# Attention and a selective scan on one core: GpSimd's products by pairs, the convolution spread over the step, the layer norm's scale and bias in the output projection, and two slots for its rstd

## The chip, the cores and the metric

The kernel runs on one core of a Trainium2 chip. Its time is the device time of one execution in microseconds; lower is better. The core has TensorE (PE, with its weight loads as PEld), VectorE (DVE), ScalarE (ACT), GpSimd (POOL), and SyncE (SP), which here issues all DMAs.

## What is computed

Two residual layers on an image batch `x` of 2 x 256 x 256 pixels with 128 channels, all in float32. Each begins with a group norm. The first is attention along the columns of the image. The second is a 3 x 3 convolution with a state space scan over all 65536 pixels of an image in row order; it takes most of the time and is what the change touches:

```python
def _L1_conv_ref(x, in_proj_w, conv_w, conv_b, x_proj_w, dt_w, dt_b, A_logs, Ds, ln_g, ln_b, out_proj_w):
    D_MODEL, D_INNER, D_STATE, DT_RANK = (128, 256, 16, 8)
    ...
    xz = x @ in_proj_w.T
    xi, z = jnp.split(xz, 2, axis=-1)
    xi = conv_3x3_depthwise(xi, conv_w) + conv_b
    xi = jax.nn.silu(xi)
    xs = xi.reshape(B, D_INNER, L)
    x_dbl = jnp.einsum('bdl,cd->bcl', xs, x_proj_w[0])
    dts, Bs, Cs = x_dbl[:, :8], x_dbl[:, 8:24], x_dbl[:, 24:]
    dts = jnp.einsum('brl,dr->bdl', dts, dt_w[0])
    delta = jax.nn.softplus(dts + dt_b[0][None, :, None])
    A = -jnp.exp(A_logs)
    y = selective_scan(xs, delta, A, Bs, Cs, Ds)
    # h = exp(delta * A) * h + (delta * xs) * B;  y = sum over 16 states of h * C, plus Ds * xs
    y = transpose_to_channels_last(y)
    mu, var = mean_and_variance(y)
    y = (y - mu) * jax.lax.rsqrt(var + 1e-05) * ln_g + ln_b
    y = y * jax.nn.silu(z)
    return y @ out_proj_w.T
```

(The convolution, the transposition and the moments are shown by names, and `x_dbl` is cut in one line.) Both layers add their result to their input.

## The kernel before

The attention stage runs first and leaves its result `x1` in HBM, one tensor for each image. The scan stage follows.

**Steps and units.** A *step* `k` is four image rows of one image, 1024 pixels (`R = 4`, `T = 1024`); there are 128, 64 for each image. In a step the scan has 256 channels x 16 states, that is 4096 recurrences, done 128 at a time: a *unit* has 32 channels (`q`, four of them in a half `h` of the channels) times 4 states (`m`, four groups), so a step has `NU = 32` units, and unit `t` is `(k, h, m, q)` with `q` running fastest. For each unit:

- `drive`: GpSimd multiplies `du` (delta times xs, spread to 128 partitions) by `bb` (the B rows, repeated) into `hb`;
- `decay`: ScalarE takes the exponential of `delta_r` times `a_neg` into `da`, in PSUM; two such tiles alternate, `da0` and `da1`;
- `scan`: VectorE runs the recurrence over 1024 pixels with `da` and `hb`, beginning from the last column that the step before left in `state`;
- `product`: the result times `cc` (the C rows), into `yc`. VectorE does it, but for the units of the tuple `POOLED`, where GpSimd does; there the scan writes into `hb` instead of `da`, since GpSimd reads no PSUM in this kernel;
- `remember`: ScalarE copies the last column to `state`;
- `add_up`, once for four units: TensorE sums the states of each channel with `sel`, into the PSUM tile `y`, where it has put `Ds * xs` at the beginning of a half; `y_out` copies `y` out at the end of a half.

**What feeds and follows it.** `project(k)` prepares step `k`: rows of `x1` are loaded (`raw`), transposed and normalised into `xn` (six rows, padded), convolved by nine accumulating matmuls for each of four blocks (`conv`, 512 pixels of one half of the channels each), gated (`gate`: z), and passed through silu, the x-projection (`states`), the dt-projection (`size`) and softplus; `times` multiplies delta by xs. `xs`, `delta`, `du`, `sz` and the B and C rows go to HBM and come back in the layouts of the units. `finish(k)` takes the step's four rows one by one: transposition and centring in one matmul (`turn`), sum of squares (`stats`), rstd on GpSimd (`scales`), `norm`, transposition back (`back`), the layer norm's scale and bias (`affine`), the product with silu(z) (`gated`, the one VectorE operation of a row), the output projection with the residual (`mix`) and the copy out (`leave`).

**Order.** The order on PE, ACT, DVE and POOL is written out by hand: a loop runs over slots `t`, one for each unit, and issues in each slot the pieces of the unit and then those pieces of `project` and `finish` that `at(t, piece)` has put there. In slot `t` these are `drive(t + 2)`, the GpSimd product of `t - 1` if it is pooled, `decay(t + 1)`, `scan(t)`, VectorE's product of `t`, `add_up(t - 5)` when its turn has come, the slot's pieces in the order in which they were put there, and `remember(t)`. SP is not in this order: the tile framework orders the DMAs that it issues. Every engine works its own queue strictly in order, so a piece that waits holds what stands behind it. In `project`, `base = k * NU - 2 * NU`: the convolution's 36 matmuls stand in slots 2 to 17 of a step, three to a slot, silu of xs in slot 21, the projections in slots 22 to 28, softplus in 29, silu of z in slot 1 of the next. The rows of `finish` begin at slots 3, 11, 19, 27 and put one piece in each slot.

**Buffers.** Tiles come from pools; a pool named `s3` has three buffers for each name. A tile whose buffers are all taken makes its writer wait for the last reader of the oldest. Here `bb` and `cc` have three, `xres` and `szr` two, `hb`, `delta_r` and `du_r` five, `yc` eight.

```python
    def pooled(t):
        return t % NU in POOLED
    ...
            if 0 <= t + 2 < end:
                drive(t + 2)
            if 0 <= t - 1 < end and pooled(t - 1):
                product(t - 1)
            if 0 <= t + 1 < end:
                decay(t + 1)
            if 0 <= t < end:
                scan(t)
                if not pooled(t):
                    product(t)
```

Of the kernel before, what the change touches and what calls it, by code (L numbers as in the profile page):

```python
# [15 lines left out]
P = 128  # L16
# [5 lines left out]
def attn_then_ssm_kernel(  # L22
# [92 lines left out]
    w_out = const.tile([P, NH, P], F32, name="w_out")  # L115
# [15 lines left out]
    with tc.tile_pool(name="prep", bufs=1) as prep, tc.tile_pool(  # L131
# [47 lines left out]
        for h in range(NH):  # L179
# [5 lines left out]
            transposed(w_out[:, h, :], outp[:, h * P : (h + 1) * P], P)  # L185
# [85 lines left out]
    with ExitStack() as actx:  # L271
# [207 lines left out]
        def gather(to, b, stats, layer):  # L479
            to[b] = group_stats(stats, ap, ps, f"{layer}_{b}", "t0")  # L480
# [102 lines left out]
    POOLED = (4, 7, 10, 13, 16, 19, 24, 26, 31)  # L583
    s1 = ctx.enter_context(tc.tile_pool(name="s1", bufs=1))
    s2 = ctx.enter_context(tc.tile_pool(name="s2", bufs=2))
    s3 = ctx.enter_context(tc.tile_pool(name="s3", bufs=3))
    s5 = ctx.enter_context(tc.tile_pool(name="s5", bufs=5))
    s8 = ctx.enter_context(tc.tile_pool(name="s8", bufs=8))
# [11 lines left out]
    def at(t, piece, *args):  # L600
        slots.setdefault(t, []).append((piece, args))

    halo = {}
    given = {}

    def project(k):
# [3 lines left out]
        base = k * NU - 2 * NU  # L610
# [4 lines left out]
        def load():  # L615

            o["raw"] = s1.tile([P, R, WT, C], F32, name="raw")
            nc.sync.dma_start(
                out=o["raw"][:, 0:n],
                in_=x1[b][R * s + 1 : R * s + 1 + n].rearrange("r (t p) c -> p r t c", p=P),  # L620
            )
            if s == 0:
                o["first"] = s1.tile([P, 1, WT, C], F32, name="first")
                nc.sync.dma_start(
                    out=o["first"], in_=x1[b][0:1].rearrange("r (t p) c -> p r t c", p=P)
                )

        def begin():


            xn = o["xn"] = s1.tile([P, R + 2, WP], F32, name="xn")
            nc.gpsimd.memset(xn[:, :, 0:1], 0.0)
            nc.gpsimd.memset(xn[:, :, WP - 1 : WP], 0.0)
            if s == 0:
                nc.gpsimd.memset(xn[:, 0, :], 0.0)
                turn("first", 0, 1)
                normalise(1, 1)
            else:
                nc.gpsimd.tensor_copy(xn[:, 0:2, 1 : W + 1], halo.pop(k - 1))
            if n < R:  # L640
                nc.gpsimd.memset(xn[:, 2 + n, :], 0.0)
# [9 lines left out]
        def normalise(to, m):  # L651
            nc.scalar.activation(
                o["xn"][:, to : to + m, 1 : W + 1],
# [6 lines left out]
        def keep():  # L660
            if s + 1 < NSTEP:
                halo[k] = s2.tile([P, 2, W], F32, name="keep")
                nc.gpsimd.tensor_copy(halo[k], o["xn"][:, R : R + 2, 1 : W + 1])

        def conv(h, i, dy):
            if dy == 0:
                o["u"] = ps_p.tile([P, RB, W], F32, name="u_ps", tag="p")
            for dx in range(3):
                nc.tensor.matmul(  # L669
                    o["u"],  # L670
                    w_tap[:, h, 3 * dy + dx, :],
                    o["xn"][:, i * RB + dy : i * RB + dy + RB, dx : dx + W],
                    start=(dy == 0 and dx == 0),
                    stop=(dy == 2 and dx == 2),
                )

        def conv_out(h, i):
            if (h, i) == (0, 0):
                o["xs"] = s1.tile([P, NH, T], F32, name="xs")
# [12 lines left out]
        def gate(h, i):  # L692
# [4 lines left out]
                o["xn"][:, 1 + i * RB : 1 + (i + 1) * RB, 1 : W + 1],  # L697
# [68 lines left out]
        at(base - 14, load)  # L766
        at(base - 4, begin)
        for r in range(0, n, RB):
            at(base - 3 + r, turn, "raw", r, min(RB, n - r))
            at(base - 2 + r, normalise, 2 + r, min(RB, n - r))  # L770
        at(base + 1, keep)
        t = base + 2
        for h in range(NH):
            for i in range(NB):
                for dy in range(3):
                    at(t + dy, conv, h, i, dy)
                at(t + 3, conv_out, h, i)
                at(t + 3, gate, h, i)
                at(t + 4, gate_out, h, i)
                t += 4  # L780
        t = base + 21
        at(t, silu_xs)
        at(t + 1, states, 0)
        at(t + 2, states_out, 0)
        at(t + 2, states, 1)
        at(t + 3, states_out, 1)
        t += 3
        for h in range(NH):
            for i in range(NB):
                at(t, size, h, i)  # L790
                at(t + 1, size_out, h, i)
                t += 1
        at(base + 29, softplus)
        at(base + 31, times, 0)
        at(base + NU, times, 1)
        at(base + NU + 1, silu_z)

    def finish(k):

        b, s = steps[k]  # L800
        for r in range(R):
            finish_row(k, b, R * s + r, r * W, (k + 1) * NU + 3 + r * (NU // R))

    def finish_row(k, b, row, t0, a):
        o = {}

        def fetch():
            o["xres"] = s2.tile([P, WT, C], F32, name="xres")
# [3 lines left out]
            o["szr"] = s2.tile([P, NH, W], F32, name="szr")  # L812
# [49 lines left out]
        def affine():  # L862
            for h in range(NH):
                nc.scalar.activation(  # L864
                    o["yd"][:, h, :],
                    o["yd"][:, h, :],
                    AF.Identity,
                    bias=lnb_c[:, h : h + 1],
                    scale=lng_c[:, h : h + 1],
                )  # L870

# [4 lines left out]
        def mix():  # L876
            o["o"] = ps_f.tile([P, WT, C], F32, name="o1_ps", tag="f")
            nc.tensor.matmul(o["o"], ident, o["xres"], start=True, stop=False)  # L878
            for j in range(WT):
                for h in range(NH):  # L880
                    nc.tensor.matmul(  # L881
                        o["o"][:, j, :],
                        o["yg"][:, h, j * P : (j + 1) * P],
                        w_out[:, h, :],
                        start=False,
# [194 lines left out]
```

## Time and profile before

| | |
|---|---|
| Time, median of 3 runs | 16465.56 us (16444.59 to 16481.3) |
| Profiled execution, its own time | 16465.48 us |
| Span of its instructions | 16463.4 us |
| First scan begins, last begins | 2690.5 us, 16402.8 us |
| Busy share of the span: DVE, POOL, PE, ACT | 90%, 83%, 83%, 67% |
| Busy from 2700 to 16400 us (13700 us): DVE, POOL, PE, ACT | 13193.7, 13336.8, 11200.3, 9583.1 us |
| Mean granted TensorE clock | 0.909; from 2700 to 16400 us 0.90 |
| DMA share of the 16 engines, 2700 to 16400 us | 0.67, 231 GB/s |

How to read it: busy rows by slice give tenths of 40 equal slices of the span (9 is 90% or more), `PEclk` the granted TensorE clock in tenths. A group line gives source line, engine, operation, what is written from what, shape and count, then the busy time in us, the mean of one in ns, and the idle time before it with what ended it. A line of the order of time gives start and duration in us, engine, source line, operation, tiles, count, and in brackets the idle time of the engine before it and its releaser. A line of waits gives who waited for whom, the us in total, how often, and the longest. A line of a stretch gives its bounds and length in us, and for PE, PEld, DVE, ACT and POOL the busy us and the number of instructions, then clock, DMA share and GB/s. Recorded durations of neighbours overlap by some hundredths of a microsecond, so distances between starts are the better measure of what one costs.

The time to landing of the loads that matter here, at the median: `bb` 4.2 us, `cc` 5.3, `delta_r` 5.6, `du_r` 4.1 (512 KB each), `xr` 7.2 (512 KB), `szr` 5.0 (256 KB), `xres` 3.7 (128 KB).

### The profile page before, as it was taken

The numbers are of one execution on the slowest core, as the hardware profiler recorded it, in microseconds if no ns is written. First come the engines' busy times: TensorE is split into PE (matmuls) and PEld (weight loads), VectorE is DVE, ScalarE is ACT, GpSimd is POOL, SyncE is SP. The second block draws the span as 40 slices with busy tenths as digits, with TensorE's granted clock in tenths as the row PEclk, the third lists the DMA queues.
The fourth block names the chain that finished last, engine by engine and source line by source line (L and its number), as shares of the span: only waits on it lengthen the run. The fifth ranks groups of instructions, "written<-read, shape, count | busy, mean of one in ns | idle before, by whom it ended". The sixth has DMA issues, their size and how long they took to land. (4 is left out here: it accounts for less than half of the span.)

```text
span 16463.4 us, 177150 instructions
## 1 busy us (share of the span) xinstructions
PE 13687.6 (83%) x55353; PEld 6810.9 (41%) x55353; DVE 14807.3 (90%) x12607; ACT 11039.0 (67%) x19870; POOL 13686.2 (83%) x7308
## 2 busy tenths in 40 slices
PE   6999997888888888888888888888888888888886
PEld 5777873333333333333333333333333333333333
DVE  7665555999999999999999999999999999999998
ACT  3555554677776677766777766777776767777665
POOL 0111114999999999999999999999999999999998
PEclk9999998888899888889998889999889998889997
DMA  4322224666666666666666666666666666666665
GB/s 186 131 86 88 82 83 146 232 234 230 232 234 230 233 232 232 233 229 232 233 233 231 233 228 232 232 235 231 230 229 230 234 234 231 233 230 234 230 231 171
DMA packets 1428932, 3452.05 MB, mean 210 GB/s; under 512 B 119784, under 2 KB 711184, under 8 KB 1407504
## 3 DMA queue, kind: packets, MB, share of 16 engines
q1 hardware_dynamic: 1427984, 3440.73, 60.6%
q8 instruction: 434, 7.11, 0.2%
q14 instruction: 514, 4.21, 0.1%
HBM read 2752.41 MB, written 687.88 MB: 209 GB/s over the span
## 5 line engine op out<-in xcount | busy, mean ns | idle before, releaser
L952 POOL TENSOR_TENSOR hb<-du_r,bb 128x1024 f32<-128x1024 f32 x4096 | 9575.1, 2363 | 0.0
L959 DVE TENSOR_TENSOR_SCAN da<-da,state,hb 128x1024 f32<-128x1024 f32 x2944 | 6903.2, 2345 | 327.8 <-ACT da L944 321.8
L944 ACT ACTIVATE da<-delta_r,a_neg 128x1024 f32<-128x1024 f32 x4096 | 4576.8, 1117 | 88.6 <-ACT state L964 0.8
L669 PE MATMUL u_ps<-xn,w_tap 128*128 128x512 f32 x9216 | 4230.3, 604 | 181.8 <-ACT state L964 168.2
L971 DVE TENSOR_TENSOR yc<-da,cc 128x1024 f32<-128x1024 f32 x2944 | 3604.7, 1224 | 254.9 <-DVE da L959 5.0
L971 POOL TENSOR_TENSOR yc<-hb,cc 128x1024 f32<-128x1024 f32 x1152 | 2719.6, 2361 | 203.0 <-issue 166.6
L959 DVE TENSOR_TENSOR_SCAN hb<-da,state,hb 128x1024 f32<-128x1024 f32 x1152 | 2697.3, 2341 | 72.6 <-ACT da L944 72.5
L991 PE MATMUL y<-yc,sel 128*32 128x512 f32 x16384 | 2527.4, 682 | 236.6 <-POOL yc L971 229.9
L669 PEld LDWEIGHTS u_ps<-xn,w_tap 128*128 128x128 f32 x9216 | 1718.3, 193 | 2190.5 <-issue 1781.4
L428 POOL TENSOR_TENSOR x1g<-xc,bo_all 128x512 f32<-128x512 f32 x256 | 315.9, 1273 | 1841.6 <-DVE stats L477 1839.7
L964 ACT COPY state<-da 128x1 f32<-128x1 f32 x2944 | 459.6, 156 | 1527.6 <-DVE yc L971 1525.8
L991 PEld LDWEIGHTS y<-yc,sel 128*32 128x32 f32 x16384 | 496.8, 116 | 1937.6 <-issue 1117.5
L821 PE MATMUL yt<-centre,ys 128*128 128x256 f32 x4096 | 1072.2, 407 | 218.4 <-ACT ob L891 217.4
L680 ACT ACTIVATE xs<-u_ps,cb_c 128x512 f32<-128x512 f32 x512 | 351.9, 687 | 1257.3 <-PE u_ps L669 977.9
L856 PE MATMUL yd<-ident,yn 128*128 128x128 f32 x2048 | 403.4, 331 | 906.5 <-ACT yn L845 877.5
L378 ACT ACTIVATE e<-s_ps,nmx 128x256 f32<-128x256 f32 x1024 | 477.6, 476 | 967.3 <-DVE nmx L369 955.1
L717 PE MATMUL xd_ps<-xs,w_xp 128*64 128x512 f32 x1024 | 683.5, 805 | 479.6 <-ACT state L964 374.8
L821 PEld LDWEIGHTS yt<-centre,ys 128*128 128x128 f32 x4096 | 794.2, 200 | 602.7 <-ACT ob L891 379.2
L735 PE MATMUL dt_ps<-xd,w_dt 8*128 8x512 f32 x1024 | 693.6, 761 | 270.7 <-ACT xd L730 263.9
L856 PEld LDWEIGHTS yd<-ident,yn 128*128 128x128 f32 x2048 | 291.2, 169 | 1263.8 <-ACT yn L845 916.2
L345 DVE TENSOR_TENSOR v<-v_ps,bv_all 128x512 f32<-128x512 f32 x256 | 177.0, 691 | 592.0 <-PE v_ps L338 592.0
L881 PEld LDWEIGHTS o_ps<-w_out,yg 128*128 128x128 f32 x4096 | 626.8, 219 | 41.4
(131 smaller groups left out, 17289.1 us busy)
## 6 DMA issues: line engine op xcount, KB each, us to landing
bb<-bc_d SPq DMA_DIRECT2D x1024, 512.0 KB, 4.2
cc<-bc_d SPq DMA_DIRECT2D x1024, 512.0 KB, 5.3
delta_r<-delta_d SPq DMA_DIRECT2D x1024, 512.0 KB, 5.6
du_r<-du_d SPq DMA_DIRECT2D x1024, 512.0 KB, 4.1
xs_d<-xs SPq DMA_DIRECT2D x128, 1024.0 KB, 6.9
xr<-xs_d SPq DMA_DIRECT2D x256, 512.0 KB, 7.2
delta_d<-delta SPq DMA_DIRECT2D x128, 1024.0 KB, 6.9
du_d<-xs SPq DMA_DIRECT2D x256, 512.0 KB, 3.2
```

Of the source, the lines that this page charges most:

```text
L378: nc.scalar.activation(e[:, i, :], o["s", r][:, i, :], AF.Exp, bias=o["nmx", r][:, i : i + 1], scale=SM, accum_out=o["den"][:, r, i : i + 1],)
L669: nc.tensor.matmul(o["u"], w_tap[:, h, 3 * dy + dx, :], o["xn"][:, i * RB + dy : i * RB + dy + RB, dx : dx + W], start=(dy == 0 and dx == ...
L717: nc.tensor.matmul(o["xd_ps"], w_xp[:, h, :], o["xs"][:, h, i * TB : (i + 1) * TB], start=(h == 0), stop=(h == NH - 1),)
L735: nc.tensor.matmul(o["dt"], w_dt[:, h, :], o["xd"][0:DR, i * TB : (i + 1) * TB], start=True, stop=True,)
L821: nc.tensor.matmul(o["yt"][:, j, :], ys[k, h][:, t0 + j * P : t0 + (j + 1) * P], centre[:, (1 - h) * P : (1 - h) * P + DI], start=(h == 0) ...
L856: nc.tensor.transpose(o["yd"][:, h, j * P : (j + 1) * P], o["yn"][:, j, h * P : (h + 1) * P], ident,)
L881: nc.tensor.matmul(o["o"][:, j, :], o["yg"][:, h, j * P : (j + 1) * P], w_out[:, h, :], start=False, stop=(j == WT - 1 and h == NH - 1),)
L944: nc.scalar.activation(da, spreads["delta", k, h, q], AF.Exp, scale=a_neg[:, g, m : m + 1])
L952: nc.gpsimd.tensor_tensor(hb, spreads["du", k, h, q], repeats["bb", k, h, m], ALU.mult)
L959: nc.vector.tensor_tensor_scan(u["h"], u["da"], u["hb"], st, ALU.mult, ALU.add)
L971: eng.tensor_tensor(u["yc"], u["h"], repeats["cc", k, h, m], ALU.mult)
L991: nc.tensor.matmul(y[q * CQ : (q + 1) * CQ, cols], sel, units[t + q]["yc"][:, cols], start=False, stop=(m == NSG - 1),)
```

## The change

**Pairs.** `POOLED` now names the first units of five pairs, so ten units of a step have their product on GpSimd instead of nine. GpSimd's drives are issued for two units at once (2048 elements a partition, `bb` and `cc` broadcast over the pair), in odd slots three units ahead, and its products for two units at once, two slots after the pair's first. `hb` and `du_r` become tiles of a pair with three buffers, `yc` of a pair with four; the buffers of `bb` and `cc` go from three to two.

**Timetable.** `base` is `k * NU - 72`. Each of the four convolution blocks gets eight slots: three, three, two and one of its nine matmuls in four successive slots, its copy out two slots later. Gates, projections and silus are put elsewhere: in slots of the step, silu of z in 21, silu of xs in 29, softplus in 13, `times` in 15 and 16. A slot's pieces are now kept in two lists, and those marked `pe=True` are issued after the others; `add_up` comes after both, a slot later than before, and `y_out` two slots later. `xn` is one tile for all steps; its two halo rows are copied by ScalarE within it, in place of two GpSimd copies by way of `keep`.

**Rows.** A row's slots begin at multiples of eight. `norm` comes two slots after `scales` instead of one. `affine` is gone: `w_out` holds the output weights twice, once times the layer norm's scale and once times its bias, and `mix` adds two matmuls for each block, `yg` with the first and silu(z) with the second. `xres` and `szr` have one buffer instead of two.

In the attention stage one call takes its small tiles from another pool.

```diff
-    w_out = const.tile([P, NH, P], F32, name="w_out")
+    w_out = const.tile([P, 2, NH, P], F32, name="w_out")
...
-            transposed(w_out[:, h, :], outp[:, h * P : (h + 1) * P], P)
+            for i, by in enumerate((lng_c, lnb_c)):
+                transposed(w_out[:, i, h, :], outp[:, h * P : (h + 1) * P], P)
+                nc.vector.tensor_scalar(
+                    w_out[:, i, h, :], w_out[:, i, h, :], by[:, h : h + 1], None, ALU.mult
+                )
...
-    POOLED = (4, 7, 10, 13, 16, 19, 24, 26, 31)
+    POOLED = (2, 6, 10, 18, 26)
...
-        base = k * NU - 2 * NU
+        base = k * NU - 72
...
-        def conv(h, i, dy):
-            if dy == 0:
+        def conv(h, i, taps):
+            if taps[0] == 0:
...
-        t = base + 2
-        for h in range(NH):
-            for i in range(NB):
-                for dy in range(3):
-                    at(t + dy, conv, h, i, dy)
-                at(t + 3, conv_out, h, i)
-                at(t + 3, gate, h, i)
-                at(t + 4, gate_out, h, i)
-                t += 4
-        t = base + 21
-        at(t, silu_xs)
...
-        at(base + 29, softplus)
-        at(base + 31, times, 0)
-        at(base + NU, times, 1)
-        at(base + NU + 1, silu_z)
+        CY = NU // 4
+        for c in range(4):
+            h, i = divmod(c, NB)
+            t = base + c * CY + 3
+            for dt, taps in ((0, (0, 1, 2)), (1, (3, 4, 5)), (2, (6, 7)), (3, (8,))):
+                at(t + dt, conv, h, i, taps, pe=True)
+            at(t + 5, conv_out, h, i)
+        for t, (h, i) in ((2, (0, 0)), (24, (0, 1)), (25, (1, 0)), (26, (1, 1))):
+            at(base + t, gate, h, i, pe=True)
+            at(base + t + 1, gate_out, h, i)
+        at(base + 29, silu_z)
+        at(base + 37, silu_xs)
+        for t, i in ((40, 0), (41, 1)):
+            at(base + t, states, i, pe=True)
+            at(base + t + 1, states_out, i)
+        for t, (h, i) in ((42, (0, 0)), (48, (1, 0)), (49, (0, 1)), (50, (1, 1))):
+            at(base + t, size, h, i, pe=True)
+            at(base + t + 1, size_out, h, i)
+        at(base + 53, softplus)
+        at(base + 55, times, 0)
+        at(base + 56, times, 1)
...
-            finish_row(k, b, R * s + r, r * W, (k + 1) * NU + 3 + r * (NU // R))
+            finish_row(k, b, R * s + r, r * W, (k + 1) * NU + (r + 1) * (NU // R))
...
-        def affine():
-            for h in range(NH):
-                nc.scalar.activation(
-                    o["yd"][:, h, :],
-                    o["yd"][:, h, :],
-                    AF.Identity,
-                    bias=lnb_c[:, h : h + 1],
-                    scale=lng_c[:, h : h + 1],
-                )
...
+                    for i, by in enumerate(("yg", "szr")):
+                        nc.tensor.matmul(
+                            o["o"][:, j, :],
+                            o[by][:, h, j * P : (j + 1) * P],
+                            w_out[:, i, h, :],
...
-        for i, piece in enumerate(
-            (turn, stats, scales, norm, back, affine, gated, mix, leave)
-        ):
-            at(a + i, piece)
+        for i, piece in (
+            (0, turn),
+            (1, stats),
+            (2, scales),
+            (4, norm),
+            (5, back),
+            (6, gated),
+            (7, mix),
+            (8, leave),
+        ):
+            at(a + i, piece, pe=piece in (turn, back, mix))
...
-                tl = repeats[name, k, h, m] = s3.tile([P, T], F32, name=name)
+                tl = repeats[name, k, h, m] = s2.tile([P, T], F32, name=name)
...
+        hb = s3.tile([P, 2, T], F32, name="hb")
+        units[t] = {"pair": hb, "hb": hb[:, 0, :]}
+        units[t + 1] = {"hb": hb[:, 1, :]}
+        nc.gpsimd.tensor_tensor(
+            hb,
+            spreads["pair", k, h, q],
+            repeats["bb", k, h, m].unsqueeze(1).to_broadcast([P, 2, T]),
+            ALU.mult,
+        )
...
+    def products(t):
+
+        k, h, m, q = unit(t)
+        hb = units[t]["pair"]
+        yc = s4.tile([P, 2, T], F32, name="yc")
+        for i in range(2):
+            units[t + i]["yc"] = yc[:, i, :]
+        nc.gpsimd.tensor_tensor(
+            yc, hb, repeats["cc", k, h, m].unsqueeze(1).to_broadcast([P, 2, T]), ALU.mult
+        )
...
-            if 0 <= t + 2 < end:
-                drive(t + 2)
-            if 0 <= t - 1 < end and pooled(t - 1):
-                product(t - 1)
+            if 0 <= t + 3 < end and t % 2:
+                drive(t + 3)
+            if 0 <= t - 2 < end and t % 2 == 0 and pooled(t - 2):
+                products(t - 2)
...
-            for piece, args in slots.pop(t, ()):
-                piece(*args)
+            for pieces in slots.pop(t, ()):
+                for piece, args in pieces:
+                    piece(*args)
+            if 0 <= t - 6 < end and (t - 6) % NQ == 0:
+                add_up(t - 6)
```

## The prediction

> **What bounds the kernel now.** I read the busy shares by slice first, then the costliest groups, then the order of time inside one step, and last who waits for whom.
>
> ```profile
> DVE  7665555999999999999999999999999999999998
> POOL 0111114999999999999999999999999999999998
> PEclk9999998888899888889998889999889998889997
> ...
> L952 POOL TENSOR_TENSOR hb<-du_r,bb 128x1024 f32<-128x1024 f32 x4096 | 9575.1, 2363 | 0.0
> ...
> L971 DVE TENSOR_TENSOR yc<-da,cc 128x1024 f32<-128x1024 f32 x2944 | 3604.7, 1224 | 254.9 <-DVE da L959 5.0
> L971 POOL TENSOR_TENSOR yc<-hb,cc 128x1024 f32<-128x1024 f32 x1152 | 2719.6, 2361 | 203.0 <-issue 166.6
> ...
> L428 POOL TENSOR_TENSOR x1g<-xc,bo_all 128x512 f32<-128x512 f32 x256 | 315.9, 1273 | 1841.6 <-DVE stats L477 1839.7
> ```
>
> From slice 7 on VectorE and GpSimd are both nine tenths busy. This is the scan stage: 128 steps of 32 units, from the first scan at 2690.5 us to the end of the last at 16405.1, 13714.6 us or 107.15 a step. GpSimd's drives (L952) never wait; its products (L971) do. To see which engine is late, I price a step from the distances between starts:
>
> ```profile
> 5009.58 2.36 DVE L959 TENSOR_TENSOR_SCAN da<-da,state,hb 128x1024 f32<-128x1024 f32 x1
> 5012.04 1.22 DVE L971 TENSOR_TENSOR yc<-da,cc 128x1024 f32<-128x1024 f32 x1
> 5013.18 2.34 DVE L959 TENSOR_TENSOR_SCAN hb<-da,state,hb 128x1024 f32<-128x1024 f32 x1
> 5015.44 2.33 DVE L959 TENSOR_TENSOR_SCAN da<-da,state,hb 128x1024 f32<-128x1024 f32 x1
> ...
> 5030.72 2.36 DVE L959 TENSOR_TENSOR_SCAN da<-da,state,hb 128x1024 f32<-128x1024 f32 x1 [1.29 <-ACT da L944]
> ...
> 5035.86 2.36 DVE L959 TENSOR_TENSOR_SCAN da<-da,state,hb 128x1024 f32<-128x1024 f32 x1 [1.45 <-ACT da L944]
> ```
>
> A unit with its product on VectorE takes 3.60 us here (3.57 averaged over a step's unpooled units), one with the product on GpSimd ("pooled") 2.26, a row's gating 0.60. VectorE: 23 x 3.57 + 9 x 2.26 + 4 x 0.60 = 104.8 us a step. GpSimd's 1024-wide products follow each other at 2.315 us; with 0.92 a row for the rstd pair, 0.57 for each halo copy and 0.1 of memsets: 43 x 2.315 + 3.7 + 1.2 = 104.5. The rest of the 107.15 is VectorE waiting for ScalarE's decay:
>
> ```profile
> DVE da L959 <- ACT da L944: 173.0, 316, 2.0
> DVE hb L959 <- ACT da L944: 72.5, 38, 2.4
> DVE yc L971 <- DVE da L959: 5.0, 11, 0.5
> ```
>
> That is 245 us, 1.9 a step; GpSimd costs VectorE 2 us in all. These stalls sit at units 29 to 31 (up to 2 us each, in 36 long steps of 108 to 112 us) and at unit 8 (0.6 us in many steps). Why is ScalarE late? In the long step above:
>
> ```profile
> 5007.05 1.93 PE L717 MATMUL xd_ps<-xs,w_xp 128*64 128x512 f32 x4 [3.07 <-ACT state L964]
> ...
> 5018.19 3.64 PE L991 MATMUL y<-yc,sel 128*32 128x512 f32 x16
> ...
> 5033.76 1.92 PE L991 MATMUL y<-yc,sel 128*32 128x512 f32 x16
> ```
> ```profile
> 5023.87 0.69 ACT L746 ACTIVATE delta<-dt_ps,dtb_c 128x512 f32<-128x512 f32 x1 [3.44 <-PE dt_ps L735]
> ```
> ```profile
> 5015.00:5030.00 15.00, 13.88 (x36) 5.72 (x36) 13.90 (x9) 7.57 (x15) 14.35 (x9) 0.50 0.63 202
> 5060.00:5105.00 45.00, 43.65 (x161) 18.63 (x163) 43.86 (x26) 26.18 (x53) 43.80 (x23) 1.00 0.67 232
> ```
>
> After the packed convolution TensorE idles (3.07 us here), its clock falls to 0.50, the same 16 matmuls take 3.64 us instead of 1.92, and ScalarE, which reads its queue in order, waits 3.44 us for a step size before it can issue the next decay. At unit 8 the opposite: TensorE has 43.65 of 45 us full of convolution, and the gate comes late. So VectorE bounds, GpSimd stands 0.3 us behind it, TensorE's timing makes the stalls.
>
> **The change, per step.** *Products.* 22 instead of 23 on VectorE: 22 x 3.57 + 10 x 2.26 + 2.4 = 103.5, 1.3 less. On GpSimd 32 drives and 10 products become 21 pairs of 2048. No such width is in the trace. From 512 to 1024 wide it goes from 1273 to 2361 ns, 2.125 ns an element, so 4.54 us; less the 0.045 by which neighbours overlap, 4.49 from start to start, against 4.63 for two singles. The ends are 4.63 (no saving) and 4.45: the Trainium skill, "GPSIMD Engine Reference", section 3.1, gives 4497 ns for a tensor_tensor of 2048 f32. I take 4.49. GpSimd: 21 x 4.49 + 2 x 2.315 + 3.7 = 102.6 (101.8 to 105.5), the halo having gone to ScalarE. Section 4.1 of that page speaks against the change: elementwise belongs on VectorE, GpSimd being about twice as slow. Its rows agree (2361 against 1224 ns) and by the rule alone a product moved loses 1.1 us; here it takes 1.3 off the later engine and the pairs pay for it.
>
> Do the pairs fit in time? Between scan 2 and scan 20 GpSimd must run 8 drives, 3 products, both `du` products and an rstd: 11 x 4.49 + 4.63 + 0.92 = 54.9; VectorE has 8 pooled and 10 plain units and 2 gatings, 55.0. It fits with nothing over; afterwards the lead grows again. An rstd or a half-speed TensorE that comes late there costs VectorE some tenths.
>
> *Convolution spread*, eight units for each of four blocks. TensorE's work at full clock is about 18.7 us in each 26 us (18 convolution passes at 0.44, `y` 1.9, `yt` 1.7, the mix now 2.3, the rest). Weighed against it: the skill's "TensorE: Matmul & The Clock Gate", section "HAM oscillation", wants the matmuls dense, since idle stretches beyond about 3.4 us drop the clock. The packed stretch at 1.00 agrees; spread too thin, all 81 us of a step at half clock would be over 160, TensorE would bind and the step with it. But its longest wait becomes some 2 us, and at 3.98 us busy of 5 the trace kept 1.00: I expect 0.97 or more, and both kinds of stall to go. I keep 0.7 us a step for what GpSimd's tight stretch and ScalarE leave: 104.2. If the cover fails, the 1.9 stay.
>
> *Scale and bias into the projection:* ScalarE loses 8 x 0.53 us a row group, 4.2 a step, and gains the 0.58 halo copy; neither is on the path, ScalarE being 70% busy. TensorE gains 16 small matmuls, 3.5 us, inside its slack. *Silus and softplus* move to units 13, 21, 29: table load, 1.91, table load, decay is 5.6 us against two plain units of 7.1 plus a gating: covered. *Rstd one unit more:* norm comes later, gating not until two units after it: nothing.
>
> *Fewer buffers.* `cc` (and `bb`) have two: SP's load of `cc` for the group after next waits for the last product before it, five times a step GpSimd's. Queued behind on SP: two or three `delta` loads, `xr`, `xres`, needed three units later. Between that product's end and VectorE's need lie one drive and one scan, 4.49 + 2.4 = 6.9 us; the load lands in 5.3 at the median: nothing. `xres`, `szr` with one buffer are fetched six units ahead, 5.0 to land: nothing.
>
> *Ends.* Before the first scan, step 1's states and sizes (2668 to 2687) move behind it: -19. In the four rows after the last scan (12.2 us each) -1.1 for the affine, +1.9 for the mix at half clock: +3. Preparing the second weight: +1.
>
> **Sum.** 128 x (104.2 - 107.15) = -378; -378 - 19 + 4 = -393. The span of 16463.4 becomes 16070; its own time is 2.1 us above it, so 16072. That execution (16465.5) stands at the median of the runs, nothing to correct.
>
> **Rivals.**
> - *GpSimd binds:* a pair costs two singles. 105.5 + 0.5: -147 - 15, 16303. For it: a broadcast operand at this width is not in the trace. Against: L428, broadcast too, shows the fixed part. 0.14.
> - *The stalls stay* (ScalarE late for another reason, or the clock stays low): 103.9 + 1.9 = 105.8, 16280. Against: every long stall has a late TensorE before it. 0.11.
> - *Slower:* `cc` lands late. Five sites a step lie 6.9 us after a GpSimd product; each microsecond beyond costs 5. From 7.5 us it eats the gain; at 8.0, 5.5 a step, 109.7 and 16775. For it: `xr`, of equal size, takes 7.2. Against: `cc` takes 5.3 with the same traffic, and a paced GpSimd gives more time than 6.9. 0.08.
> - *Hardly anything:* GpSimd's own waits (3 us a step now) come on top of 103. 0.03.
>
> My forecast has 0.64. Faster 0.88, within 0.2% (33 us, about what a measurement here tells apart) 0.03, slower 0.09. Range: low end with no stalls left (103.5) and the ends, 15980; high end takes in the first two rivals, 16310.
>
> **What would show it.** GpSimd pairs near 4.5 us; VectorE's waits for `da` under 80 us in all; granted clock at 0.97 or more; a step near 104; no `yc` on VectorE waiting for `cc`. Wrong, if drives run without a gap while scans wait for `hb` (first rival), if waits for `da` stay at 240, or if products wait for a DMA.

## The result, and the profile after

The changed kernel takes 16219.45 us (median of 4 runs, 16216.73 to 16221.97) against 16473.43 (16444.59 to 16482.11, 4 runs): ratio 0.9849, 95% interval 0.9832 to 0.9866. It is 254 us faster where 393 were forecast. The span of the profiled execution is 16220.2 us.

The page of the kernel after, busy tenths and the costliest groups:

```profile
DVE  7665555999999999999999999999999999999998
...
POOL 1111114999999999999999999999999999999998
PEclk8999998999999999999999889999999999999998
...
L957 POOL TENSOR_TENSOR hb<-du_r,bb 128x2048 f32<-128x2048 f32 x2048 | 9266.3, 4542 | 71.3 <-DMA du_r<-du_d 15.4
...
L983 DVE TENSOR_TENSOR yc<-da,cc 128x1024 f32<-128x1024 f32 x2816 | 3449.3, 1225 | 423.5 <-PE y L1014 257.4
...
L992 POOL TENSOR_TENSOR yc<-hb,cc 128x2048 f32<-128x2048 f32 x640 | 2906.7, 4542 | 62.3 <-ACT delta L747 46.8
```

The pairs last 4542 ns, drives and products alike, and GpSimd now idles 71.3 us before its drives, where it had 0.0. But the products on VectorE (L983) have 423.5 us of idle time before them where there were 254.9, most of it behind TensorE's `y`. The waits of VectorE from 2700 to 16100 us (who waited for whom, us in total, times, longest):

```profile
DVE yc L983 <- PE y L1014: 257.4, 297, 2.0
DVE da L969 <- POOL hb L957: 30.2, 98, 1.0
DVE hb L969 <- ACT da L947: 15.3, 2, 13.3
DVE yc L983 <- DMA cc<-bc_d: 11.3, 17, 1.7
```

Of the 245 us that VectorE waited for the decay, 15 are left, and 13.3 of these are one single wait, in the step that begins the second image. **In their place stands a wait that was not there: products wait for TensorE's sum.**

Between the first scan's start and the last one's end lie 13488.0 us, 105.38 a step (13714.6 and 107.15 before). I split this time into waits of VectorE (its gaps over 0.15 us, each counted whole) and the rest, its work:

| us | before | after | predicted difference | measured |
|---|---|---|---|---|
| VectorE's work in the scan stage | 13455.8 | 13168.6 | 128 x -1.3 = -166 | -287 |
| its waits there | 258.8 | 319.4 | 128 x (0.7 - 2.35) = -211 | +61 |
| up to the first scan, behind the last, preparation | 2690.5 + 58.2 | 2672.9 + 59.3 | -15 | -16.5 |
| span | 16463.4 | 16220.2 | -393 | -243 |

**Where the wait for the sum comes from.** `yc` has four pair buffers, so unit 12's product writes where units 4 and 5 wrote, and needs the sum over those to have been read: `add_up(4)`, which slot 10 issues. By the change it stands behind that slot's TensorE pieces. These end a chain of small matmuls, each of which waits until ScalarE has copied out the one before it. The order of time in a step of the kernel after (start, us, engine, line; in brackets the idle time and its releaser), TensorE first and then VectorE:

```profile
7952.98 1.92 PE L1014 MATMUL y<-yc,sel 128*32 128x512 f32 x16
...
7959.70 1.12 PE L736 MATMUL dt_ps<-xd,w_dt 8*128 8x512 f32 x2
7961.60 1.12 PE L736 MATMUL dt_ps<-xd,w_dt 8*128 8x512 f32 x2 [0.78 <-ACT delta L747]
7963.86 2.07 PE L736 MATMUL dt_ps<-xd,w_dt 8*128 8x512 f32 x2 [1.14 <-ACT delta L747]
7965.86 3.64 PE L1014 MATMUL y<-yc,sel 128*32 128x512 f32 x16
```
```profile
7961.78 4.58 DVE L969 TENSOR_TENSOR_SCAN hb<-da,state,hb 128x1024 f32<-128x1024 f32 x2
7966.28 2.33 DVE L969 TENSOR_TENSOR_SCAN da<-da,state,hb 128x1024 f32<-128x1024 f32 x1
7969.54 1.23 DVE L983 TENSOR_TENSOR yc<-da,cc 128x1024 f32<-128x1024 f32 x1 [0.93 <-PE y L1014]
```

and the same stretch by 2 us (bounds and length; busy us of PE, PEld, DVE, ACT, POOL; then the granted clock, DMA share, GB/s):

```profile
7960.00:7962.00 2.00, 1.22 (x3) 0.29 (x2) 1.97 (x3) 1.44 (x6) 1.92 (x2) 1.00 0.00 0
7962.00:7964.00 2.00, 0.86 (x3) 0.14 (x1) 2.00 (x1) 1.78 (x3) 2.00 (x1) 0.72 0.64 246
7964.00:7966.00 2.00, 2.00 (x6) 0.50 (x10) 2.00 (x2) 1.24 (x3) 1.83 (x3) 0.50 0.93 341
```

TensorE is busy for 1.22 and 0.86 of 2 us, its clock falls to 0.50, and the last pair of the chain takes 2.07 us instead of 1.12, the sum 3.64 instead of 1.92. At full clock, by my estimate, the sum would end 0.95 + 1.72 = 2.67 us earlier than 7969.50, and the product, due 2.38 us after its scan's start (7968.66), would not wait. Two scans without a product come before it (units 10 and 11 are pooled), which is why there is no slack here. The mean over the 112 steps between 3000 and 15000 us repeats this in three places: the clock is 0.53, 0.51 and 0.50 in units 11, 19 and 27, behind the step sizes, the gates, and the transpositions of new rows with a gate, and 0.96 or more in the twenty-three units outside 10 to 12, 18 to 20 and 26 to 28; units 12, 20 and 28 take 4.39, 3.89 and 4.34 us where others of their kind take 3.52 to 3.64.

### The profile page after: what moved, and what is told of

Its sections match the earlier page's. It is cut to its first block, busy times and chain, and to the rows that moved or that the text cites. A ratio compares the mean times of both kernels' runs of the same rounds, so it can differ in the third digit from the quotient of the medians.

```text
span 16220.2 us, 178642 instructions
## 1 busy us (share of the span) xinstructions
PE 14005.8 (86%) x59451; PEld 7034.3 (43%) x59451; DVE 14617.8 (90%) x12483; ACT 10627.5 (66%) x18973; POOL 13488.7 (83%) x4240
## 5 line engine op out<-in xcount | busy, mean ns | idle before, releaser
L957 POOL TENSOR_TENSOR hb<-du_r,bb 128x2048 f32<-128x2048 f32 x2048 | 9266.3, 4542 | 71.3 <-DMA du_r<-du_d 15.4
L969 DVE TENSOR_TENSOR_SCAN da<-da,state,hb 128x1024 f32<-128x1024 f32 x2816 | 6607.3, 2346 | 164.7 <-ACT da L947 131.5
L983 DVE TENSOR_TENSOR yc<-da,cc 128x1024 f32<-128x1024 f32 x2816 | 3449.3, 1225 | 423.5 <-PE y L1014 257.4
L969 DVE TENSOR_TENSOR_SCAN hb<-da,state,hb 128x1024 f32<-128x1024 f32 x1280 | 2946.7, 2335 | 15.9 <-ACT da L947 15.9
L992 POOL TENSOR_TENSOR yc<-hb,cc 128x2048 f32<-128x2048 f32 x640 | 2906.7, 4542 | 62.3 <-ACT delta L747 46.8
L695 PE MATMUL z_ps<-xn,w_z 128*128 128x512 f32 x1024 | 801.3, 875 | 696.1 <-ACT sz L706 424.0
L819 PEld LDWEIGHTS yt<-centre,ys 128*128 128x128 f32 x4096 | 744.6, 192 | 691.1 <-ACT ob L880 607.6
L870 PE MATMUL o_ps<-w_out,szr 128*128 128x128 f32 x4096 | 797.7, 277 | 0.0
L870 PE MATMUL o_ps<-w_out,yg 128*128 128x128 f32 x4096 | 796.6, 276 | 0.0
L764 POOL TENSOR_TENSOR xs<-delta,xs 128x1024 f32<-128x1024 f32 x256 | 598.7, 2364 | 98.3 <-ACT delta L755 98.3
```

Of the source, the lines that this page charges most:

```text
L695: nc.tensor.matmul(o["z"], w_z[:, h, :], xn[:, 1 + i * RB : 1 + (i + 1) * RB, 1 : W + 1], start=True, stop=True,)
L764: nc.gpsimd.tensor_tensor(du, o["delta"][:, h, :], du, ALU.mult)
L819: nc.tensor.matmul(o["yt"][:, j, :], ys[k, h][:, t0 + j * P : t0 + (j + 1) * P], centre[:, (1 - h) * P : (1 - h) * P + DI], start=(h == 0) ...
L870: nc.tensor.matmul(o["o"][:, j, :], o[by][:, h, j * P : (j + 1) * P], w_out[:, i, h, :], start=False, stop=(j == WT - 1 and h == NH - 1 an ...
L957: nc.gpsimd.tensor_tensor(hb, spreads["pair", k, h, q], repeats["bb", k, h, m].unsqueeze(1).to_broadcast([P, 2, T]), ALU.mult,)
L969: nc.vector.tensor_tensor_scan(u["h"], u["da"], u["hb"], st, ALU.mult, ALU.add)
```

## The experiments

Each is the kernel after with one edit, unless it says otherwise; ratios are to the kernel before. The kernel before itself stood between 16437 and 16482 us on the chips used, so differences of some 20 us are read from the waits, not from the ratio.

**1. The pairs taken apart:** each of GpSimd's instructions of two units becomes two of one unit, drives and products (shown) alike.

```diff
-        nc.gpsimd.tensor_tensor(
-            yc, hb, repeats["cc", k, h, m].unsqueeze(1).to_broadcast([P, 2, T]), ALU.mult
-        )
+        for i in range(2):
+            nc.gpsimd.tensor_tensor(
+                yc[:, i, :], hb[:, i, :], repeats["cc", k, h, m], ALU.mult
+            )
```

> GpSimd's pairs taken apart: drives and products as two 1024-wide instructions each, in the same slots and order. If the pair saves about 0.14 us and GpSimd stands close behind VectorE, GpSimd's step grows by 21 x 0.14 = 2.9 us to about 105.5 plus its own waits, VectorE waits for hb for over 100 us in all, and the time is 16330 to 16500. Rival: VectorE and TensorE's y alone set the step and GpSimd has 2.6 us to spare: within 30 us of 16219.

16422.47 us, 0.9981 (0.9973 to 0.9988): 203 us of the gain are the pairs. VectorE's work stays (13169.2 us); its waits in this run:

```profile
DVE yc L981 <- DMA cc<-bc_d: 283.3, 151, 4.1
DVE yc L981 <- PE y L1013: 195.0, 178, 2.2
...
DVE da L967 <- POOL hb L958: 9.1, 17, 1.0
```

GpSimd without pairs is late (106.6 us of work a step, from start to start), but this hardly shows as scans waiting for `hb`. It shows as products waiting for `cc`, most of them (239 us) in unit 28. One of these waits, SP first and then VectorE:

```profile
3919.05 0.60 SPq L933 DMA_DIRECT2D du_r<-du_d  x1
3927.90 0.51 SPq L919 DMA_DIRECT2D bb<-bc_d  x1
...
3929.65 1.53 SPq L919 DMA_DIRECT2D cc<-bc_d  x1
```
```profile
3938.95 1.23 DVE L981 TENSOR_TENSOR yc<-da,cc 128x1024 f32<-128x1024 f32 x1 [3.94 <-DMA cc<-bc_d]
```

The buffer of `cc` itself is free in good time: VectorE's product of unit 23, its last reader, starts at 3919.94. But SP stands from 3919.65 to 3927.90 at a load of `bb`, whose buffer a late drive of GpSimd still reads, and the load of `cc` is queued behind it. At the median of 100 steps it is issued 7.6 us after its own buffer came free (5.6 in the kernel after). So this is the prediction's first rival, come by the door of its third, though through `bb` and SP's queue and not, as the third had it, behind a product of GpSimd.

**2. Four pooled pairs** instead of five.

```diff
-    POOLED = (2, 6, 10, 18, 26)
+    POOLED = (2, 10, 18, 26)
```

> Four pairs instead of five (units 6 and 7 back on VectorE). If VectorE sets the step: two more products, 2 x 1.29 us a step, less the 0.24 us that it waits for hb now: some 300 us more, 16520. Rival, GpSimd sets the step: it loses 4.5 us of work a step, so faster, 16100 or less.

16503.45 us, 1.0031 (1.0019 to 1.0042). Two products more on VectorE make its work 13489.4 us, +321 or 2.51 a step (two times 1.28 is 2.56, the working being 3.53 - 2.25); waits for `hb` are gone and those for `y` stay at 261. VectorE sets the step: GpSimd has 4.7 us less to do in it, and the kernel is slower.

**3. The sum first:** `add_up` before the slot's TensorE pieces, behind the others.

```diff
-            for pieces in slots.pop(t, ()):
-                for piece, args in pieces:
-                    piece(*args)
+            acts, pes = slots.pop(t, ((), ()))
+            for piece, args in acts:
+                piece(*args)
             if 0 <= t - 6 < end and (t - 6) % NQ == 0:
                 add_up(t - 6)
+            for piece, args in pes:
+                piece(*args)
```

> add_up issued before the slot's TensorE pieces instead of behind them, same slot. If VectorE's 257 us of waiting for y come from the place behind them: these waits fall below 60 us, the time by 200 to 250 us, to about 15990. Rival: the pieces now stand behind the sum, ScalarE gets its step sizes and gates later and the waits for da return (over 100 us): within 60 us of 16219. Second rival, the sum is late because its own inputs are (GpSimd's products): waits for y unchanged.

16159.23 us (16152.93 to 16185.95), 0.9825 (0.981 to 0.9839). Its waits of VectorE:

```profile
DVE da L969 <- POOL hb L957: 71.8, 91, 1.1
DVE yc L983 <- DMA cc<-bc_d: 53.7, 84, 1.6
DVE da L969 <- ACT da L947: 47.0, 67, 1.8
DVE hb L969 <- ACT da L947: 25.0, 11, 13.9
```

No product waits for `y`: the order was the cause. (The clock rises too, to 0.944 in the scan stage and from 0.51 to 1.00 in unit 19, so this run alone does not tell the place of the sum from the clock behind which it stood; run 4 does so in part.) But of 257 us only some 60 are gained, where 200 to 250 were expected. Other waits grew by 151 (in the whole scan stage: GpSimd's drives and `cc` by 84, the decay by 57, a row's `yd` by 9), and VectorE's work by 43; units 12, 19 and 28 are still 0.4 to 0.7 us long. A faster VectorE runs into GpSimd. The prediction had given it 0.9 us a step less to do than VectorE; from start to start it has 103.6 us of work against VectorE's 102.9 in the kernel after, and it waits 87.6 us here for ScalarE's `yn` before its rstd.

**4. Fuller chains:** gates and step sizes are each issued twice, to keep TensorE busy (the second overwrites the first with the same value).

```diff
-            nc.tensor.matmul(o["dt"], w_dt[:, h, :], ..., start=True, stop=True)
+            for _ in range(2):
+                nc.tensor.matmul(o["dt"], w_dt[:, h, :], ..., start=True, stop=True)
```

> Each gate and each step-size matmul is issued twice into the same tile (the second overwrites the first with the same values), so that TensorE has more to do in the slots where its clock falls. If the half clock at units 10 to 12, 18 to 20 and 26 to 28 makes y late: clock at 0.96 or more, waits for y below 80 us, time about 16020. Rival, TensorE has simply too much before the sum: clock up or not, the waits for y grow by the added 1 us at these units, time 16300.

17007.8 us, 1.0333 (1.0318 to 1.0349): a miss in size and sign. At the gates the clock rose from 0.51 to 1.00 and unit 20 no longer waits (3.57 us). At the step sizes, matmuls of 8 rows of the array, it was 0.92, 0.51, 0.59 in units 10 to 12, no better than 0.80, 0.53, 0.61 after unit 10, and there the doubled work only lengthens the chain (unit 12: 7.24 us). In the whole scan stage the waits for `y` are 698 us and those for the decay 334. That the sum is not late at full clock is shown at one of three places, whose share of the 257 us was 45; filling with matmuls, as tried here, is no remedy.

**5. Nine taps in one slot** instead of 3, 3, 2 and 1 in four.

```diff
-            for dt, taps in ((0, (0, 1, 2)), (1, (3, 4, 5)), (2, (6, 7)), (3, (8,))):
+            for dt, taps in ((0, tuple(range(9))),):
```

> The nine matmuls of a convolution block all in the first of its four slots; everything else as in the changed kernel. If spreading them keeps TensorE fast and in time: 8 us of convolution in one slot, idle stretches after it, clock below 0.91, the waits of VectorE for y, yd or da grow from 315 us to 500 or more, time 16400 to 16700. Rival, with three quarters of its time in use TensorE absorbs it: within 60 us of 16219.

16287.44 us, 0.9899 (0.9882 to 0.9915): 68 us more, near the rival's bound. Waits for the decay stay at 15, those for `y` rise to 290 and for `cc` to 30; VectorE's work grows by 35. Spreading one block's taps over four slots is worth these 68 us, a quarter of the gain, and the stalls for the decay do not come back without it.

**6. Scale and bias back on ScalarE,** two instructions a row (the expectations of run 12 count four), in slot 6 ahead of the gating; the mix has one matmul a block instead of two, and the weights are kept once, unscaled.

```diff
             (5, back),
+            (6, affine),
             (6, gated),
```

> Scale and bias on ScalarE again (two activations for each row before the gating), one weight and half the projection's small matmuls. The prediction priced this part at nothing: within 40 us of 16219, ScalarE 4.2 us a step busier. Rival, ScalarE's in-order queue is near the path: waits for da, or of the gating for yd, over 100 us, time 16320 or more. Second rival, TensorE's 16 extra matmuls delay it: without them waits for y fall and the time is 16150 or less.

16655.63 us, 1.0122 (1.0107 to 1.0138). The gating, in the same slot, waits for them:

```profile
DVE yg L868 <- ACT yd L858: 337.1, 343, 1.2
```

This charges the edit with a wait that the kernel before did not have, where one slot lay between. **12. The same with the gating one slot later:**

```diff
-            (6, gated),
+            (6, affine),
+            (7, gated),
```

> Scale and bias of the layer norm stand again as four ScalarE instructions in slot 6, and the gating follows one slot later, in slot 7, so that VectorE does not wait for them directly; the mix has one matmul instead of two. The prediction's price for this edit, nothing: within 40 us of 16219. Rival, from the run with both in one slot (16656 us): the four instructions delay ScalarE's own queue (the decays da, the copies that free TensorE's buffers), VectorE's waits for da pass 100 us, and the time is 16300 us or more.

16248.65 us, 0.988 (0.9866 to 0.9895): 29 us more.

```profile
DVE yc L989 <- PE y L1020: 187.1, 180, 1.7
DVE hb L975 <- ACT da L953: 49.9, 45, 13.6
```

Waits for `y` fall by 70, those for the decay rise to 65, VectorE's work grows by 39. Off VectorE's path the edit costs nearly nothing; put directly ahead of VectorE it costs 436.

**7. Norm one slot after the scales,** as before.

```diff
-            (4, norm),
+            (3, norm),
```

> norm one slot after scales, as before the change, its other slots as changed. Priced at nothing: within 30 us. Rival: GpSimd's rstd stands behind a pair of 4.5 us, norm waits for it with the next decay queued behind, and VectorE waits for da at units 4, 12, 20, 28: some 0.5 us each, 2 a step, time 16400 or more.

16218.16 us, 0.9857 (0.9842 to 0.9872): no difference, no wait of VectorE moved by over 10 us. ScalarE waits 415 us for rstd in that order, and VectorE's waits for the decays behind it stay at 15.

**8. Three edits:** the sum first, the image's first row loaded seven slots earlier, and `scales` a slot later, so that GpSimd need not wait for ScalarE. (The first edit's diff is that of run 3.)

```diff
+        def load_first():
+            first = s1.tile([P, WT, C], F32, name="ob")
+            nc.sync.dma_start(
...
+        if s == 0:
+            at(base - 7, load_first)
...
-            (2, scales),
+            (3, scales),
```

> A version meant to be faster: add_up before the slot's TensorE pieces (16159 alone), the first row of an image loaded seven slots before its use instead of at its use, and GpSimd's rstd one slot later, behind its next drive. If the single wait of 13 us at the image boundary is the landing of that load: it goes (-14 us, and a few before the first scan). If GpSimd's 88 us of waiting for ScalarE's sum of squares are what now holds it: VectorE's waits for hb and cc, 126 us, fall below 60. Both: about 16070. Rival: rstd one slot later makes norm and the decays behind it late, waits for da grow, time above 16159.

16324.91 us, 0.9922 (0.9907 to 0.9936): a miss, 166 us slower than the sum alone. ScalarE now waits 497 us for rstd, the decays behind it come late (VectorE waits 317 us for `da`), and GpSimd's drives wait 253 us for scans. Run 3, with the first edit alone, has 72 us of waits for the decay, and run 10 below, with the first two and one more, 56; so it is the later scales that cost, and they have to stay where they are as long as `norm` follows in slot 4. The single wait of 13 us is gone, the longest for a decay is 1.8: it came from the load of the image's first row, which the change issues in the slot that uses it, into the one buffer that the rows' outputs leave from (`ob`). In the kernel after this load starts at 9181.86 us, when an output has landed, and TensorE stands 15.9 us until it is there; the kernel before had a tile of its own for it (`first`), loaded with the rows.

**9. Earlier first row, and `times` later** (units 21 and 25 instead of 15 and 16), the sum as in the kernel after.

```diff
-        at(base + 55, times, 0)
-        at(base + 56, times, 1)
+        at(base + 61, times, 0)
+        at(base + 65, times, 1)
```

> The same two moves (first row's load earlier, du's products at slots 61 and 65) without the column sums moved. The wait for the sum y stays at about 257 us, the wait for GpSimd's drive (30 us) and the boundary wait (13 us) go: 16170 to 16190 us. Rival: the later du delays the drives, and the time is above 16220 us.

16195.43 us (16188.79 to 16202.99): 24 less than the kernel after, 5 above what was expected. Waits for GpSimd's drives fall from 30 to 10, the boundary's is gone, `y` stands at 279.

**10. The same with the sum first,** that is with the diffs of runs 3 and 9.

> The column sums stand ahead of the slot's TensorE pieces (as in the run that took 16159 us), the image's first row is loaded seven slots earlier, and the two products that make du are moved from slots 55 and 56 of a row to slots 61 and 65, out of the stretch where GpSimd was tight. If GpSimd's tight stretch around unit 20 is what replaced the wait for the sum, the waits for GpSimd's drive and for cc (126 us together in the sum-first run) fall below 50 us and the one wait of 14 us at the image boundary goes: 16050 to 16100 us. Rival: du now lands too late for the next row's first drives, GpSimd's drives wait for the load of du_r by over 100 us in all, and the time is 16160 us or more.

16338.62 us, 0.9936 (0.9921 to 0.9951): a miss again. Drives wait no more (4.8 us), but products wait 286.9 us for `cc`, in unit 20, which takes 5.93 us. The cause is in SP's queue; the order of time of this kernel, one step:

```profile
10162.26 0.54 SPq L759 DMA_DIRECT2D delta_d<-delta  x1
10162.89 0.42 SPq L814 DMA_DIRECT2D xres<-x  x1
10168.90 0.52 SPq L940 DMA_DIRECT2D delta_r<-delta_d  x1
10169.51 0.56 SPq L926 DMA_DIRECT2D cc<-bc_d  x1
```

and of run 9, the same step:

```profile
10089.15 0.54 SPq L759 DMA_DIRECT2D delta_d<-delta  x1
10089.78 0.42 SPq L814 DMA_DIRECT2D xres<-x  x1
10090.30 1.48 SPq L926 DMA_DIRECT2D cc<-bc_d  x1
...
10095.92 0.53 SPq L940 DMA_DIRECT2D delta_r<-delta_d  x1
```

The load `delta_r` reads what `delta_d` writes, and is issued 6.6 us after it, when it has landed (6.6 at the median in this run). In run 9 `cc` stands ahead of it, in run 10 behind it. At the median of 100 steps the load of `cc` for unit 20 is issued 10.8 us after its buffer came free (5.4 in the kernel after). Nobody wrote this order: SP's is made by the framework, and moving the sums on TensorE, all in which runs 9 and 10 differ, changed it.

**11. The old timetable** of `project` (`base = k * NU - 2 * NU`, convolution packed, SiLUs and projections in their old slots), all else as in the kernel after.

```diff
-        base = k * NU - 72
+        base = k * NU - 2 * NU
...
+        t = base + 2
+        for h in range(NH):
+            for i in range(NB):
+                for dy in range(3):
+                    at(t + dy, conv, h, i, range(3 * dy, 3 * dy + 3), pe=True)
```

> Everything as changed, except that the next row's projection keeps the timetable of before: it starts four units before its own step, with packed convolution, gates and SiLUs. If the new timetable is what took away the stalls for the decays da, these return: VectorE's waits for da 150 to 260 us, granted clock 0.90 or lower, 16300 to 16450 us. Rival: the pairs, the order of the queues and the missing affine took them away; then da stays below 60 us and the time is within 60 us of 16219.

18001.05 us, 1.0947 (1.0931 to 1.0964): the rival falls, and the size is far off. VectorE waits 1260 us for the decay and 771 for `y`, and the clock is 0.862, all in the whole scan stage. TensorE and ScalarE in one place of it:

```profile
8674.06 5.49 PE L670 MATMUL u_ps<-xn,w_tap 128*128 128x512 f32 x6 [1.35 <-ACT sz L706]
8679.34 2.10 PE L1010 MATMUL y<-xr,d_diag 128*128 128x512 f32 x4
8681.37 1.92 PE L1017 MATMUL y<-yc,sel 128*32 128x512 f32 x16
```
```profile
8677.38 1.11 ACT L950 ACTIVATE da<-delta_r,a_neg 128x1024 f32<-128x1024 f32 x1
8685.74 0.37 ACT L883 COPY ob<-o_ps 128x256 f32<-128x256 f32 x1 [7.25 <-PE o_ps L873]
```

ScalarE stands 7.25 us at the copy of a row's output, because the mix lies behind packed convolution at half clock, and the next decay behind that copy. The rows at multiples of eight, the TensorE pieces issued last and the packed convolution do not go together, as far as this place shows. So this run shows that the other edits of the change do not do without the new timetable; it is no measure of what the timetable alone saves in the kernel before.

No run beats the third: 16159.23 us, the fastest version here. Not tried: the sum first with the earlier first row alone, and a third buffer of `cc` and `bb` or a fifth pair buffer of `yc`, so whether more buffers would take away the waits for `y` and `cc` stays open.

## Why the prediction came out as it did

- **Direction and bound: right, the size in part by luck.** VectorE sets the step (run 2), the decay stalls went (245 to 15 us), and the ends came within 2 us. But the waits as a whole did not fall, and some 75 us of VectorE's shorter work were not foreseen (below). Without these the time would have been near 16295 us, at the upper end of the range.
- **Pairs: right.** 4.54 us an instruction, as worked out from the slope of two widths. From start to start a drive takes 4.53 us and a product 4.62, where 4.49 was taken for both, so GpSimd has 103.6 us of work a step (102.6 predicted). "GpSimd binds" would have been true without them (run 1).
- **The stalls' end: the step that failed.** "I expect 0.97 or more, and both kinds of stall to go. I keep 0.7 us a step." The clock is 0.907 in the scan stage, and the waits are 319 us, 2.5 a step: 2.0 for `y`, 0.25 for GpSimd in its tight stretch (the "some tenths" of the prediction), 0.1 for `cc`, 0.1 for the one load. Two things were overlooked. I looked for the longest pause of TensorE (some 2 us) and expected the clock to stay up. Here no pause of TensorE from 3000 to 15000 us is over 2.7 us but one (15.9, at the change of image), and the clock falls three times a step all the same; so the Trainium skill's rule of idle stretches beyond about 3.4 us ("TensorE: Matmul & The Clock Gate", "HAM oscillation"), by which it would have stayed up, does not cover this case. The page's next section, "A second HAM failure mode: psum-queue depth-cycling", tells of frequent short pauses between groups of matmuls that pass through PSUM in turn; this is what the chains here look like, and it is the one to have weighed. And `add_up`, a slot later and behind the TensorE pieces, was read in the diff and never priced, though it frees `yc`. Run 3 shows this order to be the cause. The second rival named the low clock, but looked for its cost at the decay, with 245 us of waits left there; the cost came at `yc`. Run 3 also shows that the 257 us were not all to be had: GpSimd has no lead to give. With the sum first a step has 104.9 us (13424.8 / 128), still 0.7 above the forecast's 104.2. Two smaller slips are in the working. The step before was priced at 104.8 us of work where the trace has 105.1, so some 40 of the 211 us that were to come off the waits had never been waits. And TensorE's 18.7 us in each 26 name one of the two sums (1.9 us each) that fall in eight units; its busy time in the kernel after, weighted by the granted clock, is 81.7 us a step, 20.4 in eight units.
- **VectorE's work: right in kind, too small.** -287 against -166. The product that goes accounts for 128 x (3.58 - 2.28) = 166. Of the other 121, some 60 are a shorter distance from a scan to its product (2429 ns before, 2408 after, in the mean of products that wait for nothing; more of it in the last section) and some 15 are small gains between the other instructions. The rest, some 45, is the way of counting: an instruction that waits has its whole gap, or the overlap with its neighbour, put to the waits. Counted against the mean distances without a wait, work falls by 244 us and the waits rise by 17, from 288 to 305.
- **Scale and bias, norm's slot, two buffers of `cc`: priced at nothing, and so it was** (runs 12 and 7; 11.3 us of waits for `cc`). But the cover is less than it looks: with GpSimd late (run 1) or a different order on SP (run 10) VectorE waits 283 and 287 us for `cc`. In both its buffer was free, and the load stood behind another one in SP's queue; the prediction had looked only at the five sites behind GpSimd's products.
- **The first row's load** was not seen: 15 us, in the step where the image changes (run 8).

## What to carry to other kernels

When a stall is priced away, go on to the next thing that the same late engine releases: here TensorE's half clock no longer held the decay and held a buffer instead, and issuing the releasing instruction ahead of matmuls that wait for another engine took that wait away. Read a clock rule against the density of work in windows of a few microseconds, not only against the longest pause. After each move look at the queue that nobody wrote by hand: the loads' order on SP changed with an edit on TensorE and cost more than the edit gained, and a load whose buffer was free came late because one ahead of it was held.

## What the runs showed of the hardware

- The granted clock falls to 0.50 behind stretches in which TensorE is busy for 1.22 and 0.86 of 2 us, with pauses of 0.78 and 1.14 us. Doubling matmuls with 128 rows in such a chain brought it to 1.00; doubling those with 8 rows did not (run 4). Whether the rows decide or the chain's longer waits is open.
- A product starts 2.36 to 2.39 us after its scan's start when all that it waits for is the scan, and 2.42 to 2.46 when it also waits for TensorE's signal that the buffer of `yc` has been read, even where that signal costs no pause that the profile counts. Before, 639 of 2944 products started at 2.36 to 2.39; after, 1410 of 2816, since `yc`'s buffer is waited for once a pair. A plain unit in which nothing waits fell from 3572 to 3542 ns in the mean. This is read from the two traces; no run isolates it.
- On GpSimd a broadcast second operand costs nothing extra: 4542 ns at 2048 lies on the line through 1273 and 2361 ns at 512 and 1024.
